# Local values as seven block products per pair of key tiles, in a two-layer attention kernel

## The chip, the cores and the metric

The kernel runs on one core of a Trainium2 chip. The metric is the device time of one execution in microseconds (us), the median of three runs. A core has TensorE (matrix products; PE in the profile, its weight loads PEld), VectorE (DVE), ScalarE (ACT), GpSimd (POOL) and SyncE (SP, which issues most of the transfers). Each engine works through its own list of instructions in order; semaphores hold an instruction until the work it needs is done.

## What is computed

Two layers over images of 64 x 64 pixels with 256 channels, four images, all in float32. Layer 0 is full self-attention over the 4096 pixels of an image. Layer 1 is a depthwise 3 x 3 convolution to 768 channels, a two-layer perceptron with gelu (768 to 512 to 256), a residual sum, and a local attention in which every pixel attends to its 3 x 3 neighbours. Cut to the lines that matter here:

```python
x_out = jnp.einsum('bnm,bmc->bnc', softmax(q @ k), v)          # layer 0
perceived = conv3x3_depthwise(x)                                # layer 1
hid = gelu(einsum(perceived, w_up1) + b_up1)
h_new = x + einsum(hid, w_up2) + b_up2
qkv = jnp.einsum('bhwc,dc->bhwd', h_new, w_qkv) + b_qkv         # q, k, v
w = softmax(scores of q with the nine k around it)
out = h_new + sum over the nine positions of w * v
```

The local values that this case is about are the last third of qkv: `v = h_new @ w_v + b_v`, 256 channels in, 256 out, for every pixel.

## The kernel before

The work is cut into 32 slots (4 images x 8 blocks of 512 pixels). In slot s the kernel does full attention for block s (16 points, numbered 0 to 15; every two points cover four key tiles), the depthwise convolution for block s - 2, perceptron, guide, scores and local values for block k = s - 3 (the local values partly one slot later), and the local product of block a = s - 5. The order is written out by hand (manual schedule): at each point the loop at line 1143 issues, in this order, the energies of the next key tiles (every second point), the exponential on ScalarE (`weight`), the jobs that the list `jobs` (line 1094) has for the point, four products of weights and values (`product`, line 323), VectorE's running sum of the weights (`add_up`, line 337), and some steps of the convolution on VectorE (`share`, line 1119). At the end of a slot `partial_sums` (line 349) folds the sum of the weights into `parts`, and `finish` (line 370) takes it through a small matmul `dps` (line 376), after which the accumulators are scaled and come free. The tail after slot 31 does the last blocks by themselves.

The PSUM has eight banks: four for the energies `e`, two for the accumulators `acc`, and two that all other products share. These two are given out in turn by `job_bank` (line 108): a job takes the bank of the job before the last, and its first matmul waits until that bank has been read out.

Products of 256 x 256 blocks are already made in other places as seven block products in place of eight (two by two blocks with mixed sums, the scheme that goes back to Strassen, in Winograd's form): `hidden_part`, `update_part` and `guide_part` do it with 256 columns a product, and `gather` (line 540) or adds of their own put the products together on VectorE. `guide_part` of point 9, "ab" (lines 808 to 829), issues a copy of old guide rows on ScalarE (`guide_above`, line 774), two products into one bank, a copy of the first one by ScalarE (line 552) and an add of the second by VectorE (line 548); "cd" then takes another bank.

The local values before (`local_values`, line 887) are made per pair of key tiles (s, t): two tiles of 128 pixels, each as two matmuls of 128 x 128 by 256 columns into half a bank, four matmuls in all, and an add of the bias for each half (line 904). Key tile `keys_of(s, t, half, kin)` is a stretch of 128 pixels of h with one half of the channels, used as the stationary operand; `wlv` is the moving one. The tiles go to eight buffers of 256 columns. The first pair of block k is made at point 9, between `guide_part` "ab" and "cd", the second at point 0 of the next slot, after `hidden_part(k, 0, 0)` (products a and bc, add at line 589); `local_product` reads them at points 4 and 5 (lines 1019 to 1051).

Of the kernel before, what the change touches and what calls it, by code (L numbers as in the profile page):

```python
# [9 lines left out]
F32 = mybir.dt.float32  # L10
AF = mybir.ActivationFunctionType
ALU = mybir.AluOpType
# [3 lines left out]
P = 128  # L16
# [3 lines left out]
CH = C // P  # L20
# [32 lines left out]
def attention_then_perception_kernel(  # L53
# [37 lines left out]
    def unshifted():  # L91
# [6 lines left out]
        def tile_of(shape, tag, name, bufs=1):  # L98
            return pool.tile(shape, F32, tag=tag, name=name, bufs=bufs)
# [412 lines left out]
        lower = by_turns(range(NPC), range(LOW, TAPS), RB - 1, RB)  # L512


        wmix = pool.tile([P, 4, MULT, C], F32, tag="wmix", name="wmix")


        wmix2 = pool.tile([P, 3, CH, P], F32, tag="wmix2", name="wmix2")
        gmix = pool.tile([P, 4, P], F32, tag="gmix", name="gmix")

        def mix_weights(y11, y12, y21, y22, t1, t2, t3, t4):
# [3 lines left out]
        def blocks_of(w, kin, n):  # L525

            return [w[:, i * kin : (i + 1) * kin, bass.ts(j, n)] for i in range(2) for j in range(2)]
# [38 lines left out]
        def hidden_part(s, d, part):  # L566


            if d == 0 and part == 0:
                hids[s] = tile_of([P, NHC, NB], "hid", f"hid_{s}")  # L570

            q = hids[s].rearrange("p d (a n) -> p (d a) n", a=2)
            q11, q21, q12, q22 = 2 * d, 2 * d + 1, 2 * d + 4, 2 * d + 5
            y11, y21 = (lambda j, u=u: wup1[:, u + j, bass.ts(d, P)] for u in (0, MULT))
            y22 = lambda j: wup1[:, MULT + j, bass.ts(d + 2, P)]
            t1, t2, t3, t4 = (lambda j, i=i: wmix[:, i, j, bass.ts(d, P)] for i in range(4))

            def products(name, *todo):
                ps = job_bank(f"hid_{s}_{d}_{name}")
                for n, (w, kind) in enumerate(todo):  # L580
                    for j in range(MULT):
                        nc.tensor.matmul(  # L582
                            ps[:, n * C : (n + 1) * C], lhsT=w(j), rhs=mixes[s, j][:, kind, :],
                            start=(j == 0), stop=(j == MULT - 1),
                        )
                return ps.rearrange("p (a n) -> p a n", a=2)

            def add(to, a, b):
                nc.vector.tensor_tensor(to, a, b, ALU.add)  # L589

            def twice(t):
                return t.unsqueeze(1).to_broadcast([P, 2, C])

            if part == 0:
                nc.scalar.copy(q[:, q22, :], products("a", (y11, LOWER))[:, 0, :])
                bc = products("bc", (y21, UPPER), (t2, MIX2))
                add(q[:, q11 : q22 + 1 : q22 - q11, :], bc, twice(q[:, q22, :]))
            else:
                de = products("de", (t3, MIX3), (t1, MIX1))
                both = q[:, q21 : q12 + 1 : q12 - q21, :]  # L600
                add(both, de, twice(q[:, q22, :]))
                add(q[:, q22, :], q[:, q21, :], de[:, 1, :])
                add(both, products("gf", (t4, UPPER2), (y22, MIX4)), both)
                for i in (d, d + 2):
                    nc.scalar.activation(  # L605
                        hids[s][:, i, :], hids[s][:, i, :], AF.Gelu, bias=bup1[:, i : i + 1]
                    )
# [279 lines left out]
        def local_values(s, t):  # L887
            ps = job_bank(f"lv_{s}_{t}")
            for half in range(2):
                for kin in range(CH):  # L890
                    nc.tensor.matmul(  # L891
                        ps[:, half * C : (half + 1) * C],
                        lhsT=keys_of(s, t, half, kin), rhs=wlv[:, kin, :],
                        start=(kin == 0), stop=(kin == CH - 1),
                    )
            for half in range(2):
                if s < NSLOT - 2:
                    lvs[s, t, half] = tile_of([P, C], "lv", f"lv_{s}_{t}_{half}", 8)
                else:
                    if not half:  # L900
                        late[s, t] = late_tile(f"lv_{s}_{t}")
                    lvs[s, t, half] = late[s, t][:, half * C : (half + 1) * C]
                lv = lvs[s, t, half]
                nc.vector.tensor_tensor(lv, ps[:, half * C : (half + 1) * C], blv, ALU.add)
                if s >= NSLOT - 1:

                    square = tile_of([P, 2, NB], "den", f"lv_{s}_{t}_{half}_2")[:, 0, :C]
                    nc.gpsimd.tensor_tensor(square, lv, lv, ALU.mult)
                    watch(square)

        def pieces(s):

# [106 lines left out]
        def local_product(s, c, behind=None):  # L1019
# [30 lines left out]
            nc.vector.tensor_tensor(rv, ov, pixels(s, c), ALU.add)  # L1050
            nc.sync.dma_start(out=out[b, :, c, bass.ts(g, NB)], in_=res)

        def job(f, s, *args, n=NSLOT):
            return [lambda: f(s, *args)] if 0 <= s < n else []

# [18 lines left out]
        gbv = loaded(b_v.rearrange("o (c p) -> p (o c)", p=P), "gbv")  # L1074
        nc.vector.tensor_scalar(gbv, gbv, gam[:, 0:1], None, ALU.mult)
        wlv = pool.tile([P, CH, C], F32, tag="wlv", name="wlv")
        combine = combine_steps()


# [8 lines left out]
        for slot in range(NSLOT):  # L1088
            b, g = divmod(slot, NBLK)
            if slot >= RING:  # L1090
# [1 line left out]
            k, a = slot - LAG_HID, slot - LAG_ATT  # L1092

            jobs = [
                job(hidden_part, k, 0, 0) + job(local_values, k - 1, 1),
                job(local_denominator, a) + job(hidden_part, k, 0, 1),
                job(hidden_part, k, 1, 0), job(hidden_part, k, 1, 1),
                job(local_product, a, 0), job(local_product, a, 1) + job(update_mix, k),
                job(update_part, k, "ab"), job(update_part, k, "cd") + job(update_part, k, "eg"),
                job(update_part, k, "f"),  # L1100
                job(guide_part, k, "ab") + job(local_values, k, 0) + job(guide_part, k, "cd"),
                job(guide_part, k, "eg") + job(guide_part, k, "f"), job(scores, k, 0),
                job(scores, k, 1) + job(local_sum, k - 1), job(border_terms, k), job(border, k), [],
            ]
            if slot in (1, 2):
                jobs[0] = [lambda: next(combine)] * 2
# [13 lines left out]
            if slot == NSLOT - 1:  # L1120

                nc.sync.dma_start(out=wup2[:, :CH, P:], in_=w_up2[:, :CH, P:])


                jobs = [
                    job(hidden_part, k, 0, 0) + job(local_values, k - 1, 1),
                    job(local_denominator, a) + job(hidden_part, k, 0, 1),
                    job(hidden_part, k, 1, 0), job(hidden_part, k, 1, 1) + job(local_product, a, 0),
                    job(update, k, 0), job(update, k, 1) + job(local_product, a, 1),
                    job(guide, k, 0) + job(local_values, k, 0),  # L1130
                    job(guide, k, 1) + job(local_values, k, 1),
                    job(scores, k, 0) + job(hidden_part, k + 1, 0, 0),
                    job(scores, k, 1) + job(local_sum, k - 1) + job(hidden_part, k + 1, 0, 1),
                    job(hidden_part, k + 1, 1, 0) + job(local_total, a + 1)
                    + job(local_reciprocal, a + 1),
                    job(hidden_part, k + 1, 1, 1), job(update, k + 1, 0) + job(border, k),
                    job(local_product, a + 1, 0) + job(update, k + 1, 1),
                    job(local_product, a + 1, 1) + job(local_values, k + 1, 0),
                    job(local_values, k + 1, 1),
                ]  # L1140
                conv = chain(conv, perceive(slot - 1, upper))
                n_steps += NPC * (TAPS - 1)
            for point in range(points):
# [30 lines left out]
                if slot == 0 and point == NG:  # L1174

                    next(combine)
                    blqk = loaded(b_lqk, "blqk")
                    wperc = loaded(w_perc, "wperc")
                    bperc = loaded(b_perc, "bperc")
                    wup1 = loaded(w_up1, "wup1")  # L1180
                    bup1 = loaded(b_up1, "bup1")
                    wup2 = loaded(w_up2, "wup2")
                    mix_weights(
                        *blocks_of(wup1, MULT, C), *(wmix[:, i] for i in range(4))
                    )
                    y = blocks_of(wup2, CH, P)
                    mix_weights(*y, wmix2[:, 0], wmix2[:, 1], y[1], wmix2[:, 2])
                    bup2 = loaded(b_up2, "bup2")
                    nc.sync.dma_start(out=wlv, in_=w_qkv[:, :, 2 * C :])
                    blv = loaded(b_lv.partition_broadcast(P), "blv", [P, C])  # L1190
                if nxt and half == 1:
                    for do in nxt[G]:
                        do()
                    if slot and G + 2 < NBLK:
                        fetch(slot + 1 + G + 2)
# [470 lines left out]
```

## Time and profile before

| what | value |
|---|---|
| time, median of 3 runs | 3458.51 us (3458.17 to 3459.95) |
| time of the profiled execution | 3457.81 us |
| its span, first to last instruction | 3455.9 us |
| granted TensorE clock | 0.999 |
| PE busy | 3442.0 us (100%) |
| PEld busy | 1995.0 us (58%) |
| DVE busy | 2736.2 us (79%) |
| ACT busy | 1063.8 us (31%) |
| POOL busy | 355.7 us (10%) |

A row of the groups names the line, the engine, the operation, what it writes and reads, and the shape of each; then come the busy time of all, the mean of one in ns, and the idle time of the engine just ahead of them with what ended it. A row of the timeline has the start in us, the length in us, and the idle time before it in brackets with its releaser. A float32 matmul leaves two records in the trace, and so does its weight load. Ends of matmul records are modelled and overlap the next start, so the distance from start to start is what a record costs. A slot takes 102.1 us where nothing but its own work lies in it, and some 137 us where the next image's projections are made in it.

### The profile page before, as it was taken

The page shows a single profiled execution, that of the slowest core. Times are in us where ns is not written, and L with a number is a line of the kernel's source. Part 1 is how long each engine was busy: PE and PEld are TensorE (multiplying, and loading weights), DVE is VectorE, ACT ScalarE, POOL GpSimd, SP SyncE. Part 2 cuts the span into 40 slices and gives each one's busy share as a digit, 9 for nine tenths or more (in the row PEclk, how much of TensorE's full clock was granted, in tenths as well). Part 3 has the DMA queues.
Part 4 walks back from the last instruction along what each step waited for, and adds up shares of the span by engine and source line. Part 5 has one row for each costly group of instructions (what it writes and reads, how often), then busy time and mean ns, then how long its engine had stood idle before and what let it go on. Part 6 is the DMA issues. An engine that isn't in the chain of part 4 may idle for free.

```text
span 3455.9 us, 33709 instructions
## 1 busy us (share of the span) xinstructions
PE 3442.0 (100%) x12726; PEld 1995.0 (58%) x12726; DVE 2736.2 (79%) x4439; ACT 1063.8 (31%) x1328; POOL 355.7 (10%) x525
## 2 busy tenths in 40 slices
PE   9999999999999999999999999999999999999998
PEld 5445555556555556556555555566656555555555
DVE  2388888767888888875888888887688888888885
ACT  3233333323332233333333323333233333223331
POOL 2000001110111110111001111101110011111021
PEclk9999999999999999999999999999999999999999
DMA  4000000120000000011000000001100000000000
GB/s 107 7 4 10 7 10 16 28 48 17 16 15 8 16 16 16 22 28 43 16 10 16 10 13 16 16 22 30 41 16 16 16 10 7 16 16 18 7 7 26
DMA packets 93274, 67.05 MB, mean 19 GB/s; under 512 B 65872, under 2 KB 71248, under 8 KB 92976
## 3 DMA queue, kind: packets, MB, share of 16 engines
q1 hardware_dynamic: 92432, 64.42, 6.9%
q8 instruction: 102, 1.67, 0.2%
q14 instruction: 68, 0.56, 0.1%
q10 hardware_dynamic: 672, 0.39, 0.0%
HBM read 43.62 MB, written 18.81 MB: 18 GB/s over the span
## 4 chain that ended last, share of the span: by engine, by line
PE 98%; DVE 1%; DMA 0%; SPq 0%; ACT 0%; issue 0%; ACTq 0%; POOL 0%; DVEq 0%
PE acc L323 51%; PE e L304 8%; PE hid_de L582 4%; PE hid_gf L582 4%; PE hid_bc L582 4%; PE v L270 3%; PE lv L891 3%; PE lo L1025 3%; PE s L932 3%; PE hid_a L582 3%; PE dx_ab L534 2%; PE dx_cd L534 1%; PE dx_eg L534 1%; PE hid L614 1%; PE g_cd L534 1%; PE qk L236 1%
## 5 line engine op out<-in xcount | busy, mean ns | idle before, releaser
L323 PE MATMUL acc<-p,v 128*128 128x512 f32 x4096 | 1835.0, 594 | 0.3 <-DVE o L388 0.3
L323 PEld LDWEIGHTS acc<-p,v 128*128 128x128 f32 x4096 | 768.0, 190 | 809.9 <-issue 793.0
L477 DVE SCALAR_TENSOR_TENSOR perc<-xp,wperc,perc 128x512 f32<-128x512 f32 (+2 forms) x1554 | 1101.2, 770 | 32.4 <-ACT perc L473 32.2
L312 ACT ACTIVATE p<-e 128x1024 f32<-128x1024 f32 x512 | 524.0, 1024 | 1717.5 <-PE e L304 713.3
L337 DVE TENSOR_TENSOR den<-den,p 128x1024 f32<-128x1024 f32 x480 | 586.4, 1222 | 86.5 <-ACT p L312 84.7
L957 POOL TENSOR_TENSOR lp<-lp,near 128x396 f32<-128x396 f32 x60 | 96.4, 1607 | 2490.8 <-ACT lp L952 2490.8
L304 PE MATMUL e<-qa,ka 32*128 32x512 f32 x2048 | 291.9, 640 | 0.0
L304 PEld LDWEIGHTS e<-qa,ka 32*128 32x128 f32 x2048 | 80.0, 182 | 166.2 <-issue 145.2
L582 PE MATMUL hid_de<-perc,wmix 128*128 128x256 f32 x720 | 165.2, 379 | 0.0
L582 PEld LDWEIGHTS hid_de<-perc,wmix 128*128 128x128 f32 x720 | 136.8, 190 | 43.7 <-issue 21.5
L483 DVE TENSOR_TENSOR perc<-perc 128x256 f32<-128x256 f32 x360 | 153.5, 440 | 8.2
L605 ACT ACTIVATE hid<-hid,bup 128x512 f32<-128x512 f32 x120 | 80.1, 714 | 219.4 <-DVE hid L589 219.4
L473 ACT ACTIVATE perc<-xp,bperc,wperc 128x512 f32<-128x512 f32 x192 | 145.3, 805 | 0.0
L980 POOL TENSOR_TENSOR lsum<-lsum,lp 128x99 f32<-128x99 f32 x168 | 122.3, 735 | 11.0
L1025 PEld LDWEIGHTS lo<-lp,lv 128*128 128x128 f32 x732 | 102.9, 191 | 35.1 <-issue 27.3
L891 PE MATMUL lv<-wlv,h 128*128 128x256 f32 x520 | 122.4, 379 | 0.0
L589 DVE TENSOR_TENSOR hid<-hid_bc,hid 128x512 f32<-128x512 f32 x60 | 41.5, 692 | 101.9 <-PE hid_bc L582 101.9
L270 PE MATMUL v<-wv,xc 128*128 128x256 f32 x512 | 116.3, 380 | 0.2 <-DMA wv<-in_w_v 0.2
L270 PEld LDWEIGHTS v<-wv,xc 128*128 128x128 f32 x512 | 97.0, 190 | 28.2 <-issue 15.2
L932 PEld LDWEIGHTS s<-lq,h 128*128 128x128 f32 x520 | 87.1, 188 | 37.3 <-issue 27.4
L891 PEld LDWEIGHTS lv<-wlv,h 128*128 128x128 f32 x520 | 98.7, 190 | 15.5 <-issue 2.2
L1025 PE MATMUL lo<-lp,lv 128*128 128x99 f32 (+1 forms) x732 | 107.4, 295 | 0.0
(194 smaller groups left out, 3102.5 us busy)
## 6 DMA issues: line engine op xcount, KB each, us to landing
xp<-in_x SPq DMA_DIRECT2D x30, 528.0 KB, 4.1
xc<-in_x SPq DMA_DIRECT2D x56, 256.0 KB, 3.7
out<-lo SPq DMA_DIRECT2D x56, 256.0 KB, 2.0
qa<-packed SPq DMA_DIRECT2D x124, 64.0 KB, 2.1
out<-res SPq DMA_DIRECT2D x8, 256.0 KB, 2.0
ka<-st SPq DMA_DIRECT2D x124, 16.0 KB, 1.8
packed<-st SPq DMA_DIRECT2D x31, 64.0 KB, 1.9
wup<-in_w_up SPq DMA_DIRECT2D x1, 1536.0 KB, 6.6
```

The lines of the kernel that those rows point to most:

```text
L270: nc.tensor.matmul(ps[:, i * C : (i + 1) * C], lhsT=xc[:, kin, bass.ts(2 * pair + i, P)], rhs=wv[:, kin, :], start=(kin == 0), stop=(kin = ...
L304: nc.tensor.matmul(e[:, j, :], lhsT=key[rows, :], rhs=queries[s][rows, :], start=True, stop=True,)
L312: nc.scalar.activation(p, energies[s, G][:, 2 * half : 2 * half + 2, :], AF.Exp)
L323: nc.tensor.matmul(accs[s][c], lhsT=v[:, 2 * half + i, bass.ts(c, P)], rhs=p[:, i, :], start=(first and i == 0), stop=(G == NG - 1 and hal ...
L337: nc.vector.tensor_tensor(den, den, p, ALU.add)
L477: nc.vector.scalar_tensor_tensor(acc, win, wt, acc, ALU.mult, ALU.add)
L483: nc.vector.tensor_tensor(t[:, to, :], t[:, a, :], t[:, b, :], op)
L534: nc.tensor.matmul(ps[:, n * C : (n + 1) * C], lhsT=w(j), rhs=values(j), start=(j == 0), stop=(j == kin - 1),)
L582: nc.tensor.matmul(ps[:, n * C : (n + 1) * C], lhsT=w(j), rhs=mixes[s, j][:, kind, :], start=(j == 0), stop=(j == MULT - 1),)
L891: nc.tensor.matmul(ps[:, half * C : (half + 1) * C], lhsT=keys_of(s, t, half, kin), rhs=wlv[:, kin, :], start=(kin == 0), stop=(kin == CH ...
L932: nc.tensor.matmul(ps[:, t * QR * QW : t * QR * QW + rows * QW].rearrange("p (h w) -> p h w", w=QW), lhsT=keys_of(s, t, half, kin), rhs=gu ...
L1025: nc.tensor.matmul(pv[:, rows, columns(half)], lhsT=lvs[block, t, half][:, bass.ts(c, P)], rhs=near_ws[block, half][:, t, of, :], start=(i ...
```

## The change

For the first 28 blocks, the local values of a pair of key tiles are made by seven products of 128 x 128 by 128 columns in place of four of 128 x 128 by 256 (which are eight blocks of 128 columns). The two by two blocks are: two tiles of pixels by two halves of the input channels, times two by two blocks of the weights. The mixed sums of the weights are made once, in slot 0, by GpSimd; the mixed sums of the keys are made per pair by four VectorE operations (`key_mix`), at point 14 for the first pair of block k and at point 3 of the next slot for the second. The products go to two banks (`abcd`: four, `efg`: three), and six VectorE adds put them together. The first pair now comes at point 0 of the next slot, the second at point 9 of the next slot. Values are kept in three buffers of 512 columns in place of eight of 256. One block of mixed weights is written over the plain block that only plain products need, in `wup1` as in `wlv`; in slot 31 two transfers bring the plain blocks back (`plain_hidden`, `plain_values`), and the last blocks keep the plain products, block 28's now at points 8 and 10 of slot 31.

```diff
+        lmix = pool.tile([P, 3, 1, P], F32, tag="lmix", name="lmix")
...
+        def key_mix(s, t):
+            b11, b12, b21, b22 = (keys_of(s, t, half, kin) for kin in range(CH) for half in range(2))
+            m = tile_of([P, 4, P], "keymix", f"keymix_{s}_{t}")
+            key_mixes[s, t] = m
+            for to, a, b, op in (
+                (0, b12, b22, ALU.add), (2, b11, b12, ALU.subtract),
+                (1, m[:, 0, :], b11, ALU.subtract), (3, b21, m[:, 1, :], ALU.subtract),
+            ):
+                nc.vector.tensor_tensor(m[:, to, :], a, b, op)
+
+        def local_parts(s, t):
+            b11, _, b21, b22 = (keys_of(s, t, half, kin) for kin in range(CH) for half in range(2))
+            m = key_mixes.pop((s, t))
+            m1, m2, m3, m4 = (m[:, i, :] for i in range(4))
+            y11, t3, y21, y22 = (y[:, 0] for y in blocks_of(wlv, 1, P))
+            t1, t2, t4 = (lmix[:, i, 0] for i in range(3))
+            def products(name, *todo):
+                ps = job_bank(f"lv_{s}_{t}_{name}").rearrange("p (i c) -> p i c", c=P)
+                for i, (keys, w) in enumerate(todo):
+                    nc.tensor.matmul(ps[:, i, :], lhsT=keys, rhs=w, start=True, stop=True)
+                return ps
...
+            tile = tile_of([P, NB], "lv", f"lv_{s}_{t}", 3)
...
+            abcd = products("abcd", (b11, y11), (b21, y21), (m2, t2), (m3, t3))
+            efg = products("efg", (m1, t1), (m4, y22), (b22, t4))
+            add(o[:, 3, :], abcd[:, 0, :], blv[:, :P])
+            add(o[:, :2, :], abcd[:, 1:3, :], twice(o[:, 3, :]))
+            add(o[:, 2, :], abcd[:, 3, :], o[:, 1, :])
+            add(m1, efg[:, 0, :], bias_step)
+            add(o[:, 1:4:2, :], o[:, 1:3, :], twice(m1))
+            add(o[:, 1:3, :], efg[:, 1:3, :], o[:, 1:3, :])
...
+        def plain_hidden():
+            nc.sync.dma_start(out=wup1[:, :MULT, C:], in_=w_up1[:, :MULT, C:])
+        def plain_values():
+            nc.sync.dma_start(out=wlv[:, 0, P:], in_=w_qkv[:, 0, 2 * C + P :])
...
             jobs = [
-                job(hidden_part, k, 0, 0) + job(local_values, k - 1, 1),
+                job(hidden_part, k, 0, 0) + job(local_parts, k - 1, 0),
                 job(local_denominator, a) + job(hidden_part, k, 0, 1),
-                job(hidden_part, k, 1, 0), job(hidden_part, k, 1, 1),
+                job(hidden_part, k, 1, 0), job(hidden_part, k, 1, 1) + job(key_mix, k - 1, 1),
...
-                job(guide_part, k, "ab") + job(local_values, k, 0) + job(guide_part, k, "cd"),
+                job(guide_part, k, "ab") + job(local_parts, k - 1, 1) + job(guide_part, k, "cd"),
...
-                job(scores, k, 1) + job(local_sum, k - 1), job(border_terms, k), job(border, k), [],
+                job(scores, k, 1) + job(local_sum, k - 1), job(border_terms, k),
+                job(border, k) + job(key_mix, k, 0), [],
             ]
...
                 jobs = [
-                    job(hidden_part, k, 0, 0) + job(local_values, k - 1, 1),
+                    job(hidden_part, k, 0, 0) + job(local_parts, k - 1, 0),
...
-                    job(guide, k, 0) + job(local_values, k, 0),
-                    job(guide, k, 1) + job(local_values, k, 1),
-                    job(scores, k, 0) + job(hidden_part, k + 1, 0, 0),
+                    job(guide, k, 0) + job(local_parts, k - 1, 1) + [plain_values],
+                    job(guide, k, 1),
+                    job(scores, k, 0) + job(hidden_part, k + 1, 0, 0) + job(local_values, k, 0),
...
-                    + job(local_reciprocal, a + 1),
-                    job(hidden_part, k + 1, 1, 1), job(update, k + 1, 0) + job(border, k),
+                    + job(local_reciprocal, a + 1) + job(local_values, k, 1),
+                    job(hidden_part, k + 1, 1, 1) + [plain_hidden],
+                    job(update, k + 1, 0) + job(border, k),
```

More of the change, by code (lines that the diff above doesn't have):

```diff
@@ L512, in unshifted @@
         lower = by_turns(range(NPC), range(LOW, TAPS), RB - 1, RB)
-        wmix = pool.tile([P, 4, MULT, C], F32, tag="wmix", name="wmix")
+        wmix = pool.tile([P, 3, MULT, C], F32, tag="wmix", name="wmix")
         wmix2 = pool.tile([P, 3, CH, P], F32, tag="wmix2", name="wmix2")
+        lmix = pool.tile([P, 3, 1, P], F32, tag="lmix", name="lmix")
         gmix = pool.tile([P, 4, P], F32, tag="gmix", name="gmix")
@@ L574, in hidden_part @@
             y11, y21 = (lambda j, u=u: wup1[:, u + j, bass.ts(d, P)] for u in (0, MULT))
-            y22 = lambda j: wup1[:, MULT + j, bass.ts(d + 2, P)]
-            t1, t2, t3, t4 = (lambda j, i=i: wmix[:, i, j, bass.ts(d, P)] for i in range(4))
+            t3, y22 = (lambda j, u=u: wup1[:, u + j, bass.ts(d + 2, P)] for u in (0, MULT))
+            t1, t2, t4 = (lambda j, i=i: wmix[:, i, j, bass.ts(d, P)] for i in range(3))
             def products(name, *todo):
@@ L895, in local_values @@
                     )
+            kind, n = ("qa", 2) if (s, t) == (DIRECT, 1) else ("lv", 3)
+            o = tile_of([P, NB], kind, f"lv_{s}_{t}", n) if s < NSLOT - 2 else late_tile(f"lv_{s}_{t}")
             for half in range(2):
[L897 to L903, printed above, removed]
+                lvs[s, t, half] = lv = o[:, half * C : (half + 1) * C]
                 nc.vector.tensor_tensor(lv, ps[:, half * C : (half + 1) * C], blv, ALU.add)
@@ L909, in local_values, with twice, add @@
                     watch(square)
+        key_mixes = {}
+        def key_mix(s, t):
[18 more added lines that the diff above has]
+                return ps
+            def twice(values):
+                return values.unsqueeze(1).to_broadcast([P, 2, P])
+            def add(to, a, b):
+                nc.vector.tensor_tensor(to, a, b, ALU.add)
+            tile = tile_of([P, NB], "lv", f"lv_{s}_{t}", 3)
+            for half in range(2):
+                lvs[s, t, half] = tile[:, half * C : (half + 1) * C]
+            o = tile.rearrange("p (i c) -> p i c", c=P)
+            abcd = products("abcd", (b11, y11), (b21, y21), (m2, t2), (m3, t3))
[6 more added lines that the diff above has]
+            add(o[:, 1:3, :], efg[:, 1:3, :], o[:, 1:3, :])
         def pieces(s):
@@ L1076, in unshifted @@
         wlv = pool.tile([P, CH, C], F32, tag="wlv", name="wlv")
+        bias_step = pool.tile([P, P], F32, tag="bias_step", name="bias_step")
         combine = combine_steps()
@@ L1125, in unshifted @@
                 jobs = [
-                    job(hidden_part, k, 0, 0) + job(local_values, k - 1, 1),
+                    job(hidden_part, k, 0, 0) + job(local_parts, k - 1, 0),
                     job(local_denominator, a) + job(hidden_part, k, 0, 1),
-                    job(hidden_part, k, 1, 0), job(hidden_part, k, 1, 1) + job(local_product, a, 0),
+                    job(hidden_part, k, 1, 0),
+                    job(hidden_part, k, 1, 1) + job(local_product, a, 0) + job(key_mix, k - 1, 1),
                     job(update, k, 0), job(update, k, 1) + job(local_product, a, 1),
-                    job(guide, k, 0) + job(local_values, k, 0),
-                    job(guide, k, 1) + job(local_values, k, 1),
-                    job(scores, k, 0) + job(hidden_part, k + 1, 0, 0),
+                    job(guide, k, 0) + job(local_parts, k - 1, 1) + [plain_values],
+                    job(guide, k, 1),
+                    job(scores, k, 0) + job(hidden_part, k + 1, 0, 0) + job(local_values, k, 0),
                     job(scores, k, 1) + job(local_sum, k - 1) + job(hidden_part, k + 1, 0, 1),
                     job(hidden_part, k + 1, 1, 0) + job(local_total, a + 1)
-                    + job(local_reciprocal, a + 1),
-                    job(hidden_part, k + 1, 1, 1), job(update, k + 1, 0) + job(border, k),
+                    + job(local_reciprocal, a + 1) + job(local_values, k, 1),
+                    job(hidden_part, k + 1, 1, 1) + [plain_hidden],
+                    job(update, k + 1, 0) + job(border, k),
                     job(local_product, a + 1, 0) + job(update, k + 1, 1),
@@ L1182, in unshifted @@
                     wup2 = loaded(w_up2, "wup2")
[L1183 to L1187, printed above, removed]
                     bup2 = loaded(b_up2, "bup2")
@@ L1190, in unshifted @@
                     blv = loaded(b_lv.partition_broadcast(P), "blv", [P, C])
+                    for y, mix in (
+                        (blocks_of(wup1, MULT, C), wmix), (blocks_of(wup2, CH, P), wmix2),
+                        (blocks_of(wlv, 1, P), lmix),
+                    ):
+                        mix_weights(*y, mix[:, 0], mix[:, 1], y[1], mix[:, 2])
+                    nc.gpsimd.tensor_tensor(bias_step, blv[:, P:], blv[:, :P], ALU.subtract)
                 if nxt and half == 1:
```

## The prediction

> **What bounds the kernel now.** I read the busy shares and the chain first: is there one bound, and how full is it?
>
> ```profile
> PE 3442.0 (100%) x12726; PEld 1995.0 (58%) x12726; DVE 2736.2 (79%) x4439; ACT 1063.8 (31%) x1328; POOL 355.7 (10%) x525
> PE 98%; DVE 1%; DMA 0%; SPq 0%; ACT 0%; issue 0%; ACTq 0%; POOL 0%; DVEq 0%
> ```
>
> TensorE has work in all but 14 of 3455.9 us, and is 98% of the chain. So a change pays only in TensorE time, and anything that makes TensorE wait costs its whole length. Next the groups: what the local values cost.
>
> ```profile
> L891 PE MATMUL lv<-wlv,h 128*128 128x256 f32 x520 | 122.4, 379 | 0.0
> L904 DVE TENSOR_TENSOR lv<-lv,blv 128x256 f32<-128x256 f32 x126 | 47.5, 419 | 31.6 <-PE lv L891 29.0
> L1025 PE MATMUL lo<-lp,lv 128*128 128x99 f32 (+1 forms) x732 | 107.4, 295 | 0.0
> ```
>
> Each f32 matmul leaves two records: 65 pairs of key tiles x 4 matmuls x 2 are 520. Then the timelines of the three places that the change touches. Point 9 of slot 18 (all points of one kind agree within some 10 ns from slot to slot):
>
> ```profile
> 1906.58 1.03 PE L534 MATMUL g_ab<-h,wg 128*128 128x256 f32 x4
> 1906.83 1.02 ACT L312 ACTIVATE p<-e 128x1024 f32<-128x1024 f32 x1 [3.44 <-PE acc L323]
> 1907.44 1.89 PE L891 MATMUL lv<-wlv,h 128*128 128x256 f32 x8
> 1907.74 0.50 ACT L774 COPY lq<-lq 128x384 f32<-128x384 f32 x1
> 1908.28 0.37 ACT L552 COPY lq<-g_ab 128x256 f32<-128x256 f32 x1
> 1908.79 0.48 DVE L548 SCALAR_TENSOR_TENSOR lq<-g_ab,small,lq 128x256 f32<-128x256 f32 x1
> 1909.32 0.73 PEld L534 LDWEIGHTS g_cd<-gmix,gmix 128*128 128x128 f32 x4 [0.39 <-DVE lq L548]
> 1909.32 1.13 PE L534 MATMUL g_cd<-gmix,gmix 128*128 128x256 f32 x4
> 1910.29 3.60 PE L323 MATMUL acc<-p,v 128*128 128x512 f32 x8
> ```
>
> The thing to see: job_bank has two banks. g_ab holds one and lv the other, so g_cd needs g_ab's bank back. That bank is free when L548 ends, at 1909.27, 2.69 us after g_ab began; the chain to it is all in line behind TensorE (exponential, copy of old rows, copy of a, the add). The 1.73 us of lv cover it to within 0.15 us. The start of a slot (point 0):
>
> ```profile
> 1947.62 1.89 PE L891 MATMUL lv<-wlv,h 128*128 128x256 f32 x8
> 1947.90 0.69 DVE L589 TENSOR_TENSOR hid<-hid_bc,hid 128x512 f32<-128x512 f32 x1 [0.86 <-PE hid_bc L582]
> 1949.35 1.88 PE L323 MATMUL acc<-p,v 128*128 128x512 f32 x4
> ```
>
> Here hid_bc's bank comes free at 1948.58, 0.96 us after lv began. And the end of two slots:
>
> ```profile
> 1916.05 0.42 DVE L546 TENSOR_TENSOR lq<-g_eg,lq 128x256 f32<-128x256 f32 x1 [2.23 <-PE g_eg L534]
> ...
> 1941.36 0.69 DVE L358 TENSOR_REDUCE parts<-turned 128x16 f32<-128x512 f32 x1
> 1942.33 0.30 PE L376 MATMUL dps<-parts,fold 128*128 128x32 f32 x2
> ```
> ```profile
> 1838.47 0.69 DVE L358 TENSOR_REDUCE parts<-turned 128x16 f32<-128x512 f32 x1
> 1840.17 0.30 PE L376 MATMUL dps<-parts,fold 128*128 128x32 f32 x2
> ```
>
> VectorE's last real wait is at g_eg; from there it works for 26 us without a break, and delivers parts 0.28 us (slot 18, whose block has an image edge, so border_terms issues eight operations) or 1.01 us (slot 17) before TensorE asks for them.
>
> [...]
>
> **The change, part by part.** Times are start to start.
>
> *The matmuls themselves.* Before, 8 records x 216 ns = 1.73 us a pair (1947.62 to 1949.35). After, 14 records with 128 columns. The nearest row is the local product: 1979.76 to 1981.40 is 1.64 us for 8 records of 99 and 4 of 198 columns; the first load stands open (0.10 us: dx_ab takes 1.83 us where 8 x 216 is 1.73), a record of 198 takes 0.168 us (scores: 8 in 1.34 us); (1.64 - 0.10 - 0.67)/8 = 0.109. Bounds for 128 columns: 0.107 (half of 216) and 0.12; I take 0.11. So 0.88 us for abcd, 0.66 for efg, 1.54 us in all: 0.19 us saved a pair, 56 pairs, 10 us — if nothing waits. But the pair now takes two banks, and efg must have the bank of the job ahead of abcd.
>
> *Point 0 (slots 4 to 30, 27 times).* abcd ends 0.88 after the start, the bank is free at 0.96 + 0.055 (L548's end to g_cd's start) = 1.02. Then 0.10 of open load and 0.66: 1.78 against 1.73. Cost 0.05 each, 1.4 us. VectorE's six adds end some 0.56 us later than the two did; its 2.0 us wait for the next hid_bc takes that up.
>
> *Point 9 (slots 4 to 30, 27 times).* From g_ab's start: abcd 0.86 to 1.74. efg needs g_ab's bank: free at 2.69, so efg starts at 2.75 (g_cd's old start), 1.0 us of idle TensorE, and ends at 2.75 + 0.10 + 0.66 = 3.51. g_cd needs abcd's bank, freed by the third add. The adds stand behind L548 on VectorE: the first starts at 2.21 + 0.40 = 2.61; spacing of dependent adds is duration + 0.034 (three L546 in 1.34 us): 0.325 + 0.458 + 0.29 gives 3.68, g_cd at 3.74 instead of 2.75. Cost 1.0 us each: 27 us. Bounds: 0.77 (efg alone) and 1.15 (adds 0.05 dearer each).
>
> *key_mix at point 14 (slots 3 to 30).* Four adds ahead of add_up and partial_sums, in the 26 us without a break. guide_mix is the same pattern with 256 columns and takes 1.47 us (2007.55 to 2009.02); less 4 x 0.133 is 0.94 us. Delay of dps = 0.94 + 0.055 - margin, plus up to 0.1 of open load. Margins, read from the timeline of each slot's end as the reduce's end to dps's start, over eight slots from slot 16 on: 0.94, 1.01, 0.28, 0.17, 0.80, 1.01, 0.93, and 8.7 where projections follow; delays about 0.13, 0.09, 0.81, 0.93, 0.29, 0.09, 0.15, 0: 2.5 us per eight. Slot 3 has 2.5 us of margin. Slots 4 to 30: 8 us. Bounds: 5 us (mix 0.80) and 14 (mix 1.2).
>
> *key_mix at point 3.* 0.94 us on VectorE; perc L477 waits 0.98 us for ScalarE right after it. Nothing; if that cover went, the next idle (0.76 us before dx_cd, which has 3 us of margin) takes it.
>
> *Slot 3 and slot 31.* Slot 3's point 9 loses its lv: g_cd, 3.12 us after g_ab there, can start at 0.86: -2.3 us. Slot 31 gets both pairs of block 27 and the two plain ones of 28: 2 x 1.7 + 2 x 1.73 against three plain 5.19, and about 0.3 us at point 10 where the plain pair takes hid_bc's bank: +2 us. Its VectorE work (+3.4 us) fits in its idle of 3.65 us at 3279.
>
> *The two DMAs* wait on SyncE for the last seven-product reader, ahead of output stores; readers of plain_values come over 5 us later, of plain_hidden after the slot; comparable loads land in 2 to 7 us. Nothing. The weight mixes on GpSimd in slot 0 are first read in slot 3: nothing.
>
> Sum: 1.4 + 27 + 8 - 2.3 + 2 = +36 us on the profiled 3457.81 us (span 3455.9 and 1.9 around it): 3493.9; the median of the runs, 3458.51, is 0.7 above that execution. I write 3494.
>
> **Rivals.**
> *Faster: all waits stay hidden,* 3458.5 - 10 = 3448. It needs the bank of g_ab free at 1.74 instead of 2.69, which decides from there on; only another ScalarE order or a third bank would do it. The changed program has neither: by its semaphores the fifth product waits for that very add, and ScalarE's order is as before. Chance 0.04.
> *The mixes at the slot's end are free,* because VectorE gets through them in gaps: 36 - 8, 3486. For it: seven of eight margins but two are near 0.9 us. Chance 0.21.
> *VectorE becomes a second bound:* each slot gets 4.5 us more of it (two mixes, 12 adds for 4), and if half a microsecond more of it per slot lands on TensorE (point 0's late adds reach the Gelu and the exponentials queued behind it), 36 + 14, 3508. Against: idles of 2.0, 1.0, 1.5 us stand between. Chance 0.15.
>
> **How the numbers follow.** My forecast, 3494, has 0.60; its own range 3488 to 3501. The range reaches to both slower rivals: 3484 to 3508 leaves out the faster one (0.04), half the tail of the third and a little below the second, 0.18 at most. A measurement of this kernel can tell about 0.2% (7 us) from no change. Faster 0.03, same 0.01 (the faster rival with records of 0.12 us), slower 0.96.
>
> **What would show it.** In point 9: abcd's end to efg's start about 1.0 us, g_cd 3.74 us after g_ab, L548 still at 2.21 to 2.69. In point 0: TensorE idle 0.14 us ahead of efg. Records with 128 columns 0.11 us apart. At slot ends: dps late by 0.1 to 0.9 us, most where an image edge is. Slots of 102.1 us become 103.2 to 104.1. I am wrong if efg follows abcd directly in point 9, or if the slot period does not grow.

## The result: 39 us slower, and the profile after

The median of four runs after is 3497.95 us (3497.17 to 3499.83); before, it is 3459.23 us (3458.17 to 3461.84, four runs). The ratio is 1.0113, with an interval of 1.0101 to 1.0125. The profiled execution took 3498.53 us with a span of 3496.7, against 3457.81 and 3455.9 before: 40.8 us of span to be found.

The page after, busy shares and chain:

```profile
PE 3452.5 (99%) x13062; PEld 2004.8 (57%) x13062; DVE 2861.9 (82%) x4887; ACT 1064.4 (30%) x1328; POOL 338.7 (10%) x530
PE 89%; DVE 10%; issue 1%; SPq 0%; ACT 0%; DMA 0%; ACTq 0%; POOL 0%; DVEq 0%; POOLq 0%
```

TensorE is still nearly always busy, and yet VectorE now has 10% of the chain, where it had 1%. That is how a short wait shows when it comes back in every slot: the chain that ends last leaves TensorE for VectorE's work at each of them. (The busy time of PE is not a measure of what the products cost here: ends of records are modelled, and the starts below are what counts.) The groups of the new products, one row for each shape, with the idle time ahead of them last:

```profile
L934 PE MATMUL lv_abcd<-wlv,h 128*128 128x128 f32 x224 | 34.0, 274 | 0.0
L934 PE MATMUL lv_efg<-lmix,keymix 128*128 128x128 f32 x112 | 27.3, 326 | 22.8 <-DVE lq L550 22.5 <-DVE hid L591 0.3
L934 PE MATMUL lv_efg<-wlv,keymix 128*128 128x128 f32 x112 | 21.7, 275 | 0.0
L921 DVE TENSOR_TENSOR keymix<-h 128x128 f32<-128x128 f32 x112 | 27.7, 289 | 0.0
L941 DVE TENSOR_TENSOR lv<-lv_abcd,blv 128x128 f32<-128x128 f32 x56 | 16.0, 286 | 3.5
```

All of these products but the first of efg run without idle time; that one waits 22.5 us for one releaser, the add at L550 (L548 before), which empties the bank of g_ab. TensorE's waits give the count, 27, and the longest, 1.0 us:

```profile
PE lv_efg L934 <- DVE lq L550: 22.5, 27, 1.0
PE dps L376 <- DVE parts L358: 4.1, 6, 0.8
```

The timeline of point 9 in slot 18 (start, length, idle before and its releaser; what other engines do is cut):

```profile
1923.68 1.03 PE L536 MATMUL g_ab<-h,wg 128*128 128x256 f32 x4
...
1923.93 1.02 ACT L312 ACTIVATE p<-e 128x1024 f32<-128x1024 f32 x1 [3.44 <-PE acc L323]
...
1924.54 0.61 PE L934 MATMUL lv_abcd<-wlv,h 128*128 128x128 f32 x4
1924.85 0.50 ACT L776 COPY lq<-lq 128x384 f32<-128x384 f32 x1
...
1925.10 0.88 DVE L483 TENSOR_TENSOR perc<-perc 128x256 f32<-128x256 f32 x2
...
1925.21 0.39 PE L934 MATMUL lv_abcd<-wlv,keymix 128*128 128x128 f32 x2
1925.39 0.37 ACT L554 COPY lq<-g_ab 128x256 f32<-128x256 f32 x1
...
1925.89 0.48 DVE L550 SCALAR_TENSOR_TENSOR lq<-g_ab,small,lq 128x256 f32<-128x256 f32 x1
1926.29 0.28 DVE L941 TENSOR_TENSOR lv<-lv_abcd,blv 128x128 f32<-128x128 f32 x1
...
1926.42 0.49 PE L934 MATMUL lv_efg<-lmix,keymix 128*128 128x128 f32 x2 [0.83 <-DVE lq L550]
1926.61 0.75 DVE L941 TENSOR_TENSOR lv<-lv_abcd,lv 128x256 f32<-128x256 f32 x2
...
1927.50 1.10 PE L536 MATMUL g_cd<-gmix,gmix 128*128 128x256 f32 x4
...
1928.44 1.02 PE L323 MATMUL acc<-p,v 128*128 128x512 f32 x2
```

Counted from g_ab: the add at 2.21, efg at 2.74, g_cd at 3.82 (before: 2.745), the next `acc` products at 4.76 (before: 3.71). Read together with the adds, one wait has become two in a row. First efg waits for g_ab's bank, then g_cd waits for abcd's, which three adds empty that start only behind L550. (The second wait shows from start to start: efg's six records are through 0.76 us after its start, at 3.50; the third add ends at 3.68, and g_cd starts at 3.82.)

The end of slot 18, and point 0 of slot 19:

```profile
1960.45 0.69 DVE L358 TENSOR_REDUCE parts<-turned 128x16 f32<-128x512 f32 x1
...
1961.28 0.38 PE L376 MATMUL dps<-parts,fold 128*128 128x32 f32 x2 [0.64 <-DVE parts L358]
```
```profile
1966.65 0.61 PE L934 MATMUL lv_abcd<-wlv,h 128*128 128x128 f32 x4
1966.92 0.69 DVE L591 TENSOR_TENSOR hid<-hid_bc,hid 128x512 f32<-128x512 f32 x1 [0.86 <-PE hid_bc L584]
1967.67 0.49 PE L934 MATMUL lv_efg<-lmix,keymix 128*128 128x128 f32 x2
1968.44 1.02 PE L323 MATMUL acc<-p,v 128*128 128x512 f32 x2
```

`parts` used to be ready 0.28 us before dps was due here; now TensorE waits for it. At point 0 efg starts 1.02 us after abcd and the whole pair takes 1.79 us, against 1.73 before.

### The profile page after: what moved, and what is told of

Same layout as the page of the kernel before. It is cut to its first block, busy times and chain, and to the rows that moved or that the text cites. A ratio compares the mean times of both kernels' runs of the same rounds, so it can differ in the third digit from the quotient of the medians.

```text
span 3496.7 us, 34923 instructions
## 1 busy us (share of the span) xinstructions
PE 3452.5 (99%) x13062; PEld 2004.8 (57%) x13062; DVE 2861.9 (82%) x4887; ACT 1064.4 (30%) x1328; POOL 338.7 (10%) x530
## 4 chain that ended last, share of the span: by engine, by line
PE 89%; DVE 10%; issue 1%; SPq 0%; ACT 0%; DMA 0%; ACTq 0%; POOL 0%; DVEq 0%; POOLq 0%
PE acc L323 44%; PE e L304 7%; PE hid_de L584 4%; PE hid_bc L584 4%; PE hid_gf L584 4%; PE v L270 3%; PE lo L1070 3%; PE hid_a L584 3%; DVE perc L477 2%; PE s L977 2%; DVE den L337 2%; PE dx_ab L536 2%; PE lv_efg L934 1%; PE dx_cd L536 1%; PE dx_eg L536 1%; PE hid L616 1%
## 5 line engine op out<-in xcount | busy, mean ns | idle before, releaser
L483 DVE TENSOR_TENSOR perc<-perc 128x256 f32<-128x256 f32 x360 | 154.9, 444 | 8.2
L977 PE MATMUL s<-lq,h 128*128 128x198 f32 (+1 forms) x520 | 100.2, 334 | 0.4 <-ACT lq L789 0.4
L584 PE MATMUL hid_a<-perc,wup 128*128 128x256 f32 x360 | 93.6, 396 | 0.0
L584 PEld LDWEIGHTS hid_a<-perc,wup 128*128 128x128 f32 x360 | 63.5, 189 | 51.0 <-issue 40.2
```

Of the source, the lines that this page charges most:

```text
L483: nc.vector.tensor_tensor(t[:, to, :], t[:, a, :], t[:, b, :], op)
L584: nc.tensor.matmul(ps[:, n * C : (n + 1) * C], lhsT=w(j), rhs=mixes[s, j][:, kind, :], start=(j == 0), stop=(j == MULT - 1),)
L977: nc.tensor.matmul(ps[:, t * QR * QW : t * QR * QW + rows * QW].rearrange("p (h w) -> p h w", w=QW), lhsT=keys_of(s, t, half, kin), rhs=gu ...
```

## The experiments

Theory: TensorE waits, because the pair now takes both of the shared banks at places where a bank is not yet empty (point 9 above all), and because VectorE has four more adds ahead of the end of the slot. The products themselves are cheaper. Rival to the first half: the products, their loads or the twelve adds are dear by themselves, wherever they stand. Each run below gives a median and its ratio to the kernel before; "after" is the changed kernel. Beside these runs the kernel before gave medians of 3458.0, 3458.6 and 3458.4 us, so medians from different sets can be compared to about 1 us.

**Second pair away from point 9.** The four products of the pair go to point 5 (behind `lo`, the local product), the three to point 6 (behind `dx_ab`, a product of the perceptron); the six adds go with them, and nothing else changes.

```diff
-                job(local_product, a, 0), job(local_product, a, 1) + job(update_mix, k),
-                job(update_part, k, "ab"), ...
+                job(local_product, a, 0),
+                job(local_product, a, 1) + job(local_parts, k - 1, 1, "abcd") + job(update_mix, k),
+                job(update_part, k, "ab") + job(local_parts, k - 1, 1, "efg"), ...
...
-                job(guide_part, k, "ab") + job(local_parts, k - 1, 1) + job(guide_part, k, "cd"),
+                job(guide_part, k, "ab") + job(guide_part, k, "cd"),
```

> The changed kernel with the second pair taken out of point 9 in slots 4 to 30: its abcd goes to point 5 behind the local product, its efg to point 6 behind dx_ab, so that four accumulator products stand between any two uses of a bank; the six adds go with them. Theory (two banks in turn make TensorE wait in point 9): g_ab to the accumulator products shrinks from 4.76 us to 1.73 us, as in slot 3, and points 5 and 6 grow by 0.88 and 0.66; 27 x (3.03 - 1.54) = 40 us less than the changed kernel, about 3458 us. Rival (VectorE's 4.5 us more per slot are the bound, wherever the products stand): the adds are all still there, so at most half of that comes back, 3478 us or more.

Measured: 3458.22 us, ratio 0.9998 (0.9989 to 1.0007). The same products and the same adds, 39.7 us less: the rival falls. Point 9 in this kernel's timeline:

```profile
1904.88 1.03 PE L536 MATMUL g_ab<-h,wg 128*128 128x256 f32 x4
...
1905.74 1.03 PE L536 MATMUL g_cd<-gmix,gmix 128*128 128x256 f32 x4
...
1906.60 0.59 PE L323 MATMUL acc<-p,v 128*128 128x512 f32 x1
```

g_cd follows g_ab at 0.86 us, the length of four records, with no wait: g_cd has the other bank again, and nobody asks for g_ab's bank before the late add has emptied it.

**First mix away from the end of the slot.** The changed kernel, with `key_mix(k, 0)` at point 9 behind g_cd in place of point 14.

```diff
-                job(guide_part, k, "ab") + job(local_parts, k - 1, 1) + job(guide_part, k, "cd"),
+                job(guide_part, k, "ab") + job(local_parts, k - 1, 1) + job(guide_part, k, "cd")
+                + job(key_mix, k, 0),
...
-                job(border, k) + job(key_mix, k, 0), [],
+                job(border, k), [],
```

> The changed kernel with the first pair's key_mix moved from point 14 to point 9, behind g_cd, ahead of VectorE's wait of 2.2 us for g_eg. Theory (the mix delays dps at the slot's end, 7.7 us in the trace and about 0.05 us a slot of open load after it): dps follows the last accumulator product with no gap in every slot, 9 us less, about 3489 us. Rival (the slot's end is late for another reason, the adds of point 9): no change, 3498 us. VectorE bound: no change, as the same work is done.

Measured: 3488.64 us, 1.0087 (1.007 to 1.0104), 9.3 us less than after; the two intervals just touch, so the trace has to say it. The end of slot 18 in its timeline:

```profile
1955.25 0.69 DVE L358 TENSOR_REDUCE parts<-turned 128x16 f32<-128x512 f32 x1
...
1956.22 0.30 PE L376 MATMUL dps<-parts,fold 128*128 128x32 f32 x2
```

The reduce ends 0.28 us before dps again, as before the change, and dps has no idle time; in no slot does it come later behind the last product than in the kernel before. So the four adds cost TensorE time at the slot's end, and nothing at point 9, ahead of VectorE's real wait for g_eg.

**Plain products, only one slot later**, without mixes (as in the kernel before, four products of 256 columns), to see what the move by itself costs. The second `key_mix`, the same places of slot 31 and the mixed sums of the weights, which are not shown, go as well.

```diff
-                job(hidden_part, k, 0, 0) + job(local_parts, k - 1, 0),
+                job(hidden_part, k, 0, 0) + job(local_values, k - 1, 0),
...
-                job(guide_part, k, "ab") + job(local_parts, k - 1, 1) + job(guide_part, k, "cd"),
+                job(guide_part, k, "ab") + job(local_values, k - 1, 1) + job(guide_part, k, "cd"),
...
-                job(border, k) + job(key_mix, k, 0), [],
+                job(border, k), [],
```

> The changed kernel's schedule with the four plain products of 256 columns per pair: values one slot later, three buffers of 512 columns, no mixes of keys or of their weights, the weights' other changes kept. Theory (moving the values costs nothing): as before, with slot 3 shorter by 2.3 us and slot 31 longer by about 2 us, 3459 us. Rival (something of the move itself, the buffers or the later values, is part of the loss): 3465 us or more.

Measured: 3457.43 us, 0.9998 (0.999 to 1.0007). No cost of the move is seen; in the trace slot 3 is 2.3 us shorter, slot 31 is 2.0 us longer, and the slots between keep their length.

**The same with the mixes computed and not read.** Both `key_mix` calls stand where the changed kernel has them.

```diff
-                job(border, k), [],
+                job(border, k) + job(key_mix, k, 0), [],
```

> The kernel of the run before (plain products, one slot later) with both key_mix calls kept, whose results nobody reads: the price of the mixing alone. Theory: the mix at point 14 costs 7.7 to 9 us, the one at point 3 nothing, so 3467 us. VectorE bound: twice 0.95 us a slot, 27 x 1.9 = 51 us, 3510 us. Free mixes: 3459 us.

Measured: 3466.93 us, 1.0026 (1.0016 to 1.0035): 9.5 us for the mixes alone, next to the 9.3 of the kernel above, reached from the other side. Its slot 18:

```profile
1944.13 0.69 DVE L358 TENSOR_REDUCE parts<-turned 128x16 f32<-128x512 f32 x1
...
1944.96 0.38 PE L376 MATMUL dps<-parts,fold 128*128 128x32 f32 x2 [0.64 <-DVE parts L358]
```

The line for dps is that of after, wait and all, without one block product of local values in the kernel. All of it stands at the ends of the slots, so the second mix, at point 3, costs nothing.

**Both moves together.** The edits of the first and the second kernel.

> Both moves in one kernel: the second pair's products at points 5 and 6, the first pair's key_mix at point 9. Theory: the two costs stand in different places and add up, 3498 - 40 - 9 = 3449 us, below the kernel before, as the seven products of the second pair then save their 0.19 us and point 9 loses also the 0.25 us of waiting and open load that it had before. Rival (VectorE, whose work is the same, has become the bound): the second move brings less than 5 us, 3453 us or more.

Measured: 3449.24 us, 0.9971 (0.996 to 0.9982). With neither wait the seven products gain. But part of that may be the place, so the next kernel gives the place to the plain products.

**Plain products one slot later, second pair at point 5.**

```diff
-                job(local_product, a, 0), job(local_product, a, 1) + job(update_mix, k),
+                job(local_product, a, 0),
+                job(local_product, a, 1) + job(local_values, k - 1, 1) + job(update_mix, k),
...
-                job(guide_part, k, "ab") + job(local_values, k - 1, 1) + job(guide_part, k, "cd"),
+                job(guide_part, k, "ab") + job(guide_part, k, "cd"),
```

> Plain products for all blocks, one slot later (the kernel without mixes), and the second pair moved from point 9 to point 5 behind the local product: what the place is worth by itself. Theory: point 9 goes from 3.71 us (g_ab to the accumulator products) to 1.73, point 5 grows by 1.73: 0.25 us less a slot, 27 x 0.25 = 7 us, 3451 us. So of what both moves gain against the kernel before, 7 us are the place, and the seven products of the second pair bring 27 x 0.19 = 5 us, less 27 x 0.06 = 2 us lost at point 0. Rival (the seven products save what the two moves gain, the place nothing): 3457 us.

Measured: 3450.86 us, 0.9979 (0.997 to 0.9988): 6.6 us below the same products at point 9. There the kernel before lost 0.15 us of idle time and 0.10 of open load at g_cd in each of 27 slots, 6.8 us, which the lines in the prediction hold already. What the seven products added to this place, from 3450.86 to 3449.24, is 1.6 us, which these intervals do not tell from nothing. The traces do: from dps to dps each of the 27 slots is 0.10 us shorter with the seven products, 2.7 us in all, as 0.17 saved in the second pair less 0.06 lost at point 0 would have it.

**Point 0 without a wait.** To both moves: abcd goes between the products a and bc of `hidden_part`, and efg behind bc.

```diff
+        def hidden_part(s, d, part, between=None):
...
+                if between:
+                    between()
...
-                job(hidden_part, k, 0, 0) + job(local_parts, k - 1, 0),
+                [lambda k=k: hidden_part(k, 0, 0, lambda: local_parts(k - 1, 0, "abcd"))]
+                + job(local_parts, k - 1, 0, "efg")
+                if k > 0 else job(hidden_part, k, 0, 0),
```

> As the run with both moves, and in point 0 the order a, abcd, bc, efg in place of a, bc, abcd, efg in slots 4 to 30, so that the copy of a is covered by abcd and the adds of abcd by bc. Theory (efg waits there for hid_bc's bank and has its load open): from the start of abcd's 0.88 us and efg's 0.66 us nothing is lost, 1.54 us in place of 1.79, 27 x 0.25 = 7 us less than with both moves, 3442 us. Rival: the adds of abcd come late behind the scaling of the accumulators on VectorE and efg waits for them instead, 3449 us.

Measured: 3443.22 us, 0.9953 (0.994 to 0.9967): faster than both kernels. Its point 0:

```profile
1934.48 0.61 PE L938 MATMUL lv_abcd<-wlv,h 128*128 128x128 f32 x4
...
1935.37 1.46 PE L584 MATMUL hid_bc<-perc,wup 128*128 128x256 f32 x6
...
1936.71 0.75 DVE L945 TENSOR_TENSOR lv<-lv_abcd,lv 128x256 f32<-128x256 f32 x2
...
1937.96 0.38 PE L938 MATMUL lv_efg<-lmix,keymix 128*128 128x128 f32 x2
...
1938.63 1.45 PE L323 MATMUL acc<-p,v 128*128 128x512 f32 x3
```

abcd takes 0.89 us, efg 0.67, 1.56 in all against 1.73 for the plain pair. The 2.6 us of bc lie between the two, and in them the adds empty abcd's bank. Against the plain products at point 5 the median is 7.6 us less. In the traces each of the 27 slots is 0.33 us shorter, 8.8 us in all, which is what two pairs at 0.17 save.

**What holds g_ab's bank at point 9.** The prediction named a chain: exponential, copy of old rows, copy of a, the add. Three kernels, each the changed kernel with one edit or both. First the copy of the old rows goes to point 8, out of ScalarE's queue:

```diff
-            if part == "ab":
-                guide_above(s)
...
-                job(update_part, k, "f"),
+                job(update_part, k, "f") + job(guide_above, k),
```

> The changed kernel with ScalarE's copy of old rows (0.50 us) moved from point 9 to point 8, so that it no longer stands ahead of the copy of a. Theory (the add that frees g_ab's bank stands behind two queues, ScalarE's copies until 2.08 us after g_ab's start and VectorE's convolution steps until 2.21): VectorE's queue still holds it, so nothing changes, 3498 us. Rival (ScalarE's line alone sets it, as the chain named in the prediction reads): 0.5 us less a slot, 27 x 0.5 = 13 us, 3485 us.

Measured: 3498.98 us, 1.0118 (1.0101 to 1.0135), no gain, and efg still at 2.74 us. Then two convolution steps (L483) go from point 8 to point 9, where they come behind the add:

```diff
-            share = [6, 7, 7, 5, 4, 3, 3, 3, 2, 2, 4, 5, 5, 4, 0, 0]
+            share = [6, 7, 7, 5, 4, 3, 3, 3, 0, 4, 4, 5, 5, 4, 0, 0]
```

> The changed kernel with the two convolution steps of point 8 moved to point 9, behind the add that frees g_ab's bank. Theory of two queues: ScalarE's copy ends at 2.08 and holds the add to 2.13 in place of 2.21, 0.08 us less a slot, 2 us, 3496 us. Rival (VectorE's queue alone): 0.5 us or more a slot, 3485 us or less.

Measured: 3495.65 us, 1.0108 (1.0091 to 1.0125), which is not told apart from after; efg at 2.65. And both edits:

> Both moves of the last two runs. Theory of two queues: the exponential ends at 1.27, the copy of a at 1.65, the add starts at 1.71 in place of 2.21, so efg at 2.24 and g_cd at 3.32 after g_ab: 0.5 us less a slot, 27 x 0.5 = 13.5 us, 3484 us, more than the sum of the two runs. If one queue alone set it, this run would equal one of the two.

Measured: 3481.65 us, 1.0067 (1.0051 to 1.0084), 16.3 us less than after. Its point 9:

```profile
1915.92 1.03 PE L536 MATMUL g_ab<-h,wg 128*128 128x256 f32 x4
...
1917.09 0.37 ACT L554 COPY lq<-g_ab 128x256 f32<-128x256 f32 x1
...
1917.49 0.48 DVE L550 SCALAR_TENSOR_TENSOR lq<-g_ab,small,lq 128x256 f32<-128x256 f32 x1
...
1918.03 0.49 PE L932 MATMUL lv_efg<-lmix,keymix 128*128 128x128 f32 x2 [0.19 <-DVE lq L550]
...
1919.10 1.10 PE L536 MATMUL g_cd<-gmix,gmix 128*128 128x256 f32 x4
```

The add now starts at 1.57 us in place of 2.21, and efg, g_cd and acc each come 0.63 to 0.64 earlier: 27 x 0.63 is 17. That is a little more than expected: the sum had put the copy of a behind the end of the exponential's record, at 1.27, and it starts at 1.17. In after, two queues let the add go at nearly the same time, ScalarE's copy of a at 2.08 us and VectorE's two steps at 2.21. To shorten one of them shows the other.

## Why the prediction was right, and where it was off

The forecast was 3494 us, in a range from 3484 to 3508; it came 3497.95. Its steps, from the trace after, slot by slot:

| step | predicted, us | in the trace, us |
|---|---|---|
| point 9, 27 slots | 27 (1.0 each) | 28.2 (1.05 each) |
| point 0, 27 slots | 1.4 | 1.7 |
| `key_mix` at the slot's end | 8 | 7.7, and 1.6 of open load |
| slot 3 | -2.3 | -2.3 |
| slot 31 | +2 | +2.5 |
| tail | none | +1.5 |
| sum | 36 | 40.9 (span: 40.8) |

Every step came as forecast or dearer, so between the steps no error hides another.

*Right: the bank at point 9.* efg was put at 2.75 us after g_ab and came at 2.74. g_cd was put at 3.74 and came at 3.82. The first of the three adds starts at 2.61 and the last ends at 3.68, both as said, but from there to g_cd were 0.14 us where 0.055 had been taken. g_cd's own load then stood open for 0.03 us less than before, so the next `acc` products come 1.05 us later. Moving the pair away gave it all back, and more. The bound of 1.15 held it.

*Right: the products.* Records of 128 columns are 0.11 us apart (abcd's last four start at 1924.99 and 1925.21, two by two), as taken from the rows with 99 and 198 columns, and the loads ahead of them are 0.11 us apart too (1924.88 and 1925.10 in the trace of after). That is half of the 0.216 us of a record of 256 columns, but records of 99 columns took no less, 0.109 us. Whether the load sets the pace was not shown. The gain of 10 us is nearly there when nothing waits: 8.8 us in the 27 slots, by the kernel with point 0 split.

*Right: the slot's end.* The delays of dps were 0.28, 0.07, 0.14, 0, 0.14, 0.07, 0.79 and 0.91 us (slots 4 to 11) where eight margins had said 0.29, 0.09, 0.15, 0, 0.13, 0.09, 0.81 and 0.93, each margin read from the trace before. In part that is luck: the forecast delays held up to 0.1 us of open load, and in the trace this tenth stands ahead of dps, which starts 0.15 us after the reduce's end where 0.055 had been taken. The open load behind dps, 0.06 us a slot on average, comes on top and was in no term. Two experiments, from opposite sides, give 9.3 and 9.5 us with it. The rival "the mixes at the slot's end are free" is out. The adds of `key_mix` took 0.29 us each (0.289 in the L921 row above). For 128 columns the prediction's sums put 0.29 us, and they take 0.133 off each operation of `guide_mix`, which has 256; both were the author's estimates, and two rows of the trace before bear them out:

```profile
L589 DVE TENSOR_TENSOR hid<-hid_bc,hid 128x512 f32<-128x512 f32 x60 | 41.5, 692 | 101.9 <-PE hid_bc L582 101.9
L546 DVE TENSOR_TENSOR lq<-g_cd,lq 128x256 f32<-128x256 f32 x56 | 23.7, 424 | 11.7 <-PE g_cd L534 10.7
```

256 columns fewer are 268 ns less, so 128 fewer are 134 less, and 128 columns come to 290 ns.

*Out: VectorE as a second bound.* It has 126 us more work, and slots of 102.1 us became 103.3 to 104.3, which the waits of the table account for; nothing is left over for half a microsecond more in each slot.

*Wrong: what the faster rival needs.* The prediction wrote that "only another ScalarE order or a third bank would do it". Another ScalarE order alone did nothing. VectorE's two L483 steps stand ahead of the add, which starts 0.13 us after the copy has ended. VectorE kept to that order: with only the copy of the old rows out of the way, efg stayed at 2.74 us; with the two steps moved as well, it came at 2.11. In the trace before they stand there too, from 1907.99 for 0.88 us, and the add starts at 1908.79; the prediction left them out of "the chain to it". Even with both moved, the bank comes free at about 2.05 us, not at the 1.74 that the rival asked for. The exponential, whose record ends at 1.27, and the copy and the add after it, remain. A third bank was not tried. What did take the wait away was another place for the pair (points 5 and 6), which the prediction did not think of.

*Missed: the tail.* 1.5 us is lost behind the last slot, where the change has put nothing. The windows of the last perceptron (length, then busy PE, PEld, DVE, ACT, POOL, granted clock, DMA) of after, and of before at the same work:

```profile
3428.80:3432.90 4.10, 4.10 (x9) 1.77 (x9) 4.07 (x7) 1.55 (x2) 0.24 (x1) 0.58 0.00 0
3432.90:3441.00 8.10, 8.10 (x20) 3.61 (x19) 1.39 (x3) 0.69 (x1) 0.38 (x1) 1.00 0.01 2
```
```profile
3389.45:3393.50 4.05, 4.05 (x14) 1.98 (x13) 4.05 (x7) 1.55 (x2) 0.24 (x1) 1.00 0.00 0
```

In the same 4.1 us TensorE gets through 9 records in place of 14, at a granted clock of 0.58 in place of 1.00. Whether the change brings this on is open: the profiled execution of the kernel with the pair at points 5 and 6, which runs at 3458.22 us, had a mean granted clock of 0.998, and that of the plain kernel one slot later, which runs at 3457.43, had 0.999.

## What to carry to other kernels

Count the buffers that a cheaper formula takes, not only its operations: a job that is split over both of two rotating banks makes itself wait for the job before it, and the next one wait for its adds, so here a gain of 0.17 us turned into a loss of 1.05. A split job belongs where the job between its halves is longer than the adds that empty its bank (here bc's 2.6 us, and 1.07 of adds), and added work on a side engine belongs ahead of that engine's next real wait (9.3 us here). Before you shorten the queue that holds a buffer, look for a second queue that ends at nearly the same time (here 0.13 us apart), and move both.

## What the runs showed of the hardware

In the tail of after the granted clock was 0.50 for 3.4 us (about 3429.4 to 3432.8), and the records of `hid` were then 0.85 us apart in place of 0.43. In the 5 us ahead of it TensorE had idled for 1.03 and 0.77 us (lines below), between short products for `ld` (the denominators of the local softmax). The kernel before has the same two gaps, 1.03 and 0.77 us, and its profiled execution shows a clock of 1.00 behind them; what sets the clock down was not shown. Most times of the kernel before lie in two groups, around 3457.8 and around 3459.6 us. The 3.4 us at half the clock cost 1.7 us by the author's estimate, about as much as the groups are apart; that the one makes the other was not shown.

```profile
3426.50 0.47 PE L1050 MATMUL ld<-lv,ones 128*128 128x99 f32 x2 [1.03 <-DVE lv L1004]
...
3428.32 0.46 PE L1050 MATMUL ld<-lp,ones 128*128 128x99 f32 x2 [0.77 <-DVE lp L1004]
```

A wait on TensorE cost 0.07 to 0.10 us more than its idle time here, as the first weight load behind it stood open: in the trace of after, efg's first load and first record both start at 1926.42, where abcd's first load, without a wait, starts 0.21 us ahead of its record (1924.33 and 1924.54). With the wait efg's first two records take 0.49 us where the same records without a wait (in the kernel with point 0 split) take 0.38, and from dps to the next records are 0.31 us in place of 0.23.

From the end of the VectorE operation to the first record that waited for it were 0.05 us at efg, but 0.14 to 0.15 at g_cd and dps; why they differ is open.
